# Two scanning layers on one core: the input on 128 partitions of 24 rows, kept in DRAM by position and quarter, the first eight rows placed by products, one group's input moved to a later place

## The chip, the core and the metric

The kernel runs on one core of a Trainium2 chip. The metric is the device time of one execution in microseconds (us), here the median of three runs. All data are 32-bit floats. Engines: PE multiplies matrices, DVE, ACT and POOL work element by element, SP only issues DMAs (ACT and POOL issue a few as well). Every engine takes its instructions in order, and an issuing engine stands still at a DMA whose data are not ready.

## What is computed

x has 32 images, 48 channels, 64 rows and 128 columns. There are two layers with weights of their own. Each normalizes x over 16 groups of three channels per image, runs four scans, and adds the result to x:

```
def layer(x, down, right, left):              # each a weight (48, 48, 5) and a bias
    v = (x - mean) / sqrt(var + 1e-5)         # per image and group of 3 channels, over all rows, columns
    for h in 1 .. 63:       D[h] = v[h] + conv5(D[h-1], down)          # along the columns
    U[63] = D[63]; then backwards with the same weights:
    for h in 62 .. 0:       U[h] = (D[h-1], or D[63] for h = 0) + conv5(U[h+1], down)
    for w in 1 .. 127:      R[w] = U[w] + conv5(R[w-1], right)         # along the rows
    for w in 126 .. 0:      L[w] = R[w] + conv5(L[w+1], left)
    return x + L
```

A row needs the row before it, so a scan is a chain of 63 or 127 steps. The statistics need all of an image's x before the first row can be scaled.

## The kernel before

**Groups and phases.** Eight images make a group; there are four. `PHASES` lists the order: row phases (down and up scan of one group, 126 steps) and column phases (right and left scan of two groups together, 254 steps). Twelve phases follow each other on PE without a break in the program: rows of group 0, rows of group 1, columns of both, and so on. The trace names a step by layer, group or pair, and way: `step_00d` is layer 0, group 0, down; `step_00r` layer 0, pair 0, right.

**A step** (`step`, L824) is nine matmuls (L837) over three partition groups o, and three additions on DVE (L846) that add the scan's input and the bias. In the trace a matmul is two records, so 63 steps are 1134 records. The 384 values of a row (eight positions of a column modulo 8, times 48 channels) are cut by `PIECES` into ten runs of 16 to 48 partitions. The arena holds three slots; rows 0 to 31 of a group lie in one, rows 32 to 63 in the next.

**From x to rows.** x arrives with channels and halves of the rows on 96 partitions (`PX`: channel c, half s), 32 rows on each. Bringing it into the layout of a step takes a round trip through DRAM for each row: `take_in` loads it, `permute` (L621, four copies of 96 x 256 on POOL or ACT) reorders it, `put_out` writes it to the DRAM tile `xin` in runs of 1 KB (`lines`), and `move_rows` reads it back in runs of 128 bytes, ten DMAs (one for each piece) for four or eight rows. `xin` has 96 lines, one for each partition, with 1024 elements of padding in every two of them (`PAD`), and inside a line the order is position (row modulo 8), quarter of the columns, block of eight rows. `scale_rows` (L667 on ACT, 24 instructions for four or eight rows) or `scale_at_once` (L678 on POOL) then normalize. The residual of layer 0 is read back from `xin` too (`load_residual`, runs of 4 KB).

**Statistics.** For group 0 DVE takes them (`InputStats.take`, L474, one for each 512 elements; `aggregate`, L477), for groups 1 to 3 ACT does (`take_others`, L487 and L495, sums and squares). `scaling` (L341) turns them into scale and offset with nine small matmuls on PE for x (L352, L363), a square root on ACT (L394) and a few DVE instructions.

**The start** (`first_group`, L1126) is written out by hand. It loads the first weights and builds the step's matrix from them with matmuls against shifted identities (`place_kernel`, L1180), loads group 0 in 16 pieces (two halves of the rows, eight images), takes statistics, and moves the rows. Rows 0 to 3 don't go through DRAM: `rows_by_product` (L1210) picks them from the loaded x by ten matmuls of 512 columns each with the shifted identities, and ACT copies the products from PSUM (L1217). After the scaling, `scale_first` normalizes rows 0 to 3 on DVE and ACT (L690, L692), then rows follow in the order in which `move_rows` and `scale_rows` stand. Puts and reads of `xin` alternate: rows 4 to 16 need the first half of the rows only.

**The order of everything else** is an agenda: `at(t, fn, ...)` sets work for step t, counted over all phases (`starts[k]` is a phase's first step), and `catch_up` writes it between the steps into each engine's instruction list. `in_order` keeps the instructions of an engine in the order in which they were written. `plan_input` sets the input of groups 1 to 3: for each piece of four rows a load, two permutes with their puts, and the statistics. Before, the third group's (index 2) eight pieces stand from step 16 of the first column phase on, 13.5 steps apart. The column phase holds four quarters of the columns in three slots: `plan_cols` writes quarter 0 away (`spill_unit`, steps 33 to 43 of the phase), loads quarter 3 in its place (`load_unit` with j = 3, steps 50 to 60), and reads quarter 0 back for the left scan. Nearly all these DMAs are on SP, so they stand in one line with the puts and loads of the input. Column 96 is the first of quarter 3.

Of the kernel before, what the change touches and what calls it, by code (L numbers as in the profile page):

```python
# [36 lines left out]
PX = 2 * C  # L37
# [83 lines left out]
def kernel(  # L121
# [22 lines left out]
    NBN = H * W // (2 * BN)  # L144
    CHANNEL = H * W * GB
    PAD = 1024
    WEIGHTS = NG * NG * FULL
    assert N == FULL and SLOT == NG * HALF * N and SLOT == 6 * UNIT

# [29 lines left out]
    mask_x = const([PX, PX], "mask_x")  # L179
    maskp = const([PX, NG, FULL], "maskp")  # L180
    mask_in = const([FULL, NG, C], "mask_in")
    mask_sb = mask_in[0:PX, 0]
    mask_r = const([FULL, NG, PX], "mask_r")
# [3 lines left out]
    def kept(name):  # L187
# [6 lines left out]
    MOIETY = (CHANNEL + PAD) // 2  # L194
    source = [
        [
            dram.tile([PX, MOIETY], F32, tag=f"xin{g}", name=f"xin{g}")[:, 0 : CHANNEL // 2]
# [29 lines left out]
    def x_by_row(t, e, h0, h1):  # L227

        s, h = divmod(h0, HALF)
        t = t.rearrange("(c s) (i q a e n) -> s e a c i q n", s=2, i=E8, q=NQ, a=NH // 2, e=E8)  # L230
        t = t[s, e, h // E8, :, h % E8 : h % E8 + h1 - h0]
        return t.rearrange("c i q n -> c (i q) n")

    def x_by_col(t, e, j):


        return t.rearrange("(c s) (i q n) -> i q c s n", s=2, i=E8, q=NQ)[e, j]

    def lines(t, h0, h1):

        t = t.rearrange("p (i q a n) -> a p i q n", i=E8, q=NQ, a=NH // 2)[h0 // E8]
        return t[:, h0 % E8 : h0 % E8 + h1 - h0].rearrange("p i q n -> p (i q) n")
# [70 lines left out]
    def load_masks(dma):  # L313
        for s in range(2):
            dma(sided(mask_sb)[s], mask[SIDES[s], SIDES[0]])
# [5 lines left out]
    def spread_masks():  # L321
        for s in range(2):
            nc.gpsimd.tensor_copy(mask_x.rearrange("p (c s) -> p s c", s=2)[:, s], mask_sb)
        for e, c0, c1, o, p0 in PIECES:
            nc.gpsimd.tensor_copy(maskp[:, o, p0 : p0 + c1 - c0], mask_sb[:, c0:c1])

    def spread_row_masks():
        for s in range(2):
            nc.gpsimd.tensor_scalar(
                mask_r.rearrange("p o (c s) -> p o s c", s=2)[:, :, s],  # L330
                mask_in,
                2.0 / E8,
                None,
                ALU.mult,
            )
# [5 lines left out]
    def scaling(key, layer, g, averages, masks, slack=0):  # L341
# [29 lines left out]
        average(ps[0:PX, 0], mean_p)  # L371
# [10 lines left out]
        dev = spare[0 : FULL if n > 1 else PX, 0:n]  # L382
        if not slack:
            far = ps[0:PX, 1 + NG : 2 + NG]
            nc.vector.tensor_tensor(far, mean_p, ps[0:PX, 0:1], ALU.subtract)
            nc.vector.tensor_tensor(dev, mean_p, ps[0:PX, 0:1], ALU.subtract)
# [20 lines left out]
        if n > 1:  # L407
            mean_c = stat_tile([PX, GB], "mean_c", key)
            nc.vector.tensor_copy(mean_c, ps[0:PX, 0])
            yield  # L410
            expand(mean, mean_c)
            yield
            nc.vector.tensor_tensor(dev, mean_p, mean, ALU.subtract)
            nc.vector.tensor_copy(mean_s, mean)
        else:
            nc.vector.tensor_tensor(dev, mean_p, ps[0:PX, 0:1], ALU.subtract)
# [8 lines left out]
        else:  # L425
            average(ps[0:PX, 1 + NG], dev, var_p)
            yield
            var_c = stat_tile([PX, GB], "var_c", key)
            nc.vector.tensor_copy(var_c, ps[0:PX, 1 + NG])
# [26 lines left out]
    class InputStats:  # L456
# [3 lines left out]
        def __init__(self, key, nv):  # L460
            self.nv = nv
            self.mv = stat_tile([PX, 1, GB, 2], "mv_x", key)
            if nv:
                self.st = stat_tile([PX, nv, NBN * 6], "bn", key)
            if nv < GB:
                self.sum, self.neg, self.dev2 = (
                    stat_tile([PX, GB, NBN], f"{n}_x", key)[:, nv:] for n in ("sum", "neg", "dev2")
# [11 lines left out]
        def take_others(self, i, nat):  # L479
            k = nat.shape[-1] // BN  # L480
            for square in (False, True):
                for b in range(self.nv, GB):
                    for n in range(k):
                        at = b - self.nv, slice(i + n, i + n + 1)
                        piece = nat[:, b, n * BN : (n + 1) * BN]
                        if square:
                            nc.scalar.activation(  # L487
                                junk[0:PX],
# [5 lines left out]
                        else:  # L494
                            nc.scalar.activation(  # L495
                                junk[0:PX],
# [8 lines left out]
        def __call__(self, key, slack):  # L505
# [3 lines left out]
            if self.nv < GB:  # L509
                n = GB - self.nv  # L510
                mean = stat_tile([PX, GB], "mean_x", key)[:, 0:n]
# [6 lines left out]
                    dev, dev, mean.unsqueeze(2).to_broadcast([PX, n, NBN]), ALU.add  # L518
# [7 lines left out]
                var = stat_tile([PX, GB], "var_x", key)[:, 0:n]  # L526
# [78 lines left out]
    def take_in(g, r0, nat, batches=slice(0, GB)):  # L605


        n = nat.shape[-1] // W
        src = x[g * GB : (g + 1) * GB].rearrange("b c (s h) w -> (c s) b (h w)", s=2)
        dma(nat[:, batches], src[:, batches, r0 * W : (r0 + n) * W])  # L610
# [12 lines left out]
    def put_out(g, r, perm):  # L623
# [3 lines left out]
        dma(lines(source[0][g], r, r + n), perm.rearrange("p (m n) -> p m n", n=LINE))  # L627
# [127 lines left out]
    def load_residual(k, j, i, nat):  # L755
# [3 lines left out]
        for e, c0, c1, p0 in pieces(o):  # L759
            here = nat[p0 : p0 + c1 - c0]  # L760
            if layer:
                dma(here, by_col(t, e, j)[c0:c1], nc.scalar)
            else:
                dma(here.rearrange("p (s n) -> p s n", s=2), x_by_col(t, e, j)[c0:c1])
# [336 lines left out]
    def wide_nat(i0, n):  # L1101
        return arena[0:PX, i0 : i0 + GB * n * W].rearrange("p (b m) -> p b m", b=GB)

    tiles = [stage[0:PX, i] for i in range(4)]
    nats1 = [wide_nat(2 * SLOT + i * UNIT * 2, 4) for i in range(4)]
    plan_input(1, [starts[0] + 46 + 6 * j for j in range(8)], 5, 1, nats1, tiles[2:4])
    nats = [wide_nat(3 * SLOT, 4)]
    times = [starts[2] + 16 + 13.5 * j for j in range(8)]
    plan_input(2, times, 6, 6, nats, tiles[2:4])
    times = [t + 15 * j for t in (starts[3] + 42, starts[4] + 24) for j in range(4)]  # L1110
# [5 lines left out]
    at(starts[1] + 58, load_row_masks)  # L1116
    at(starts[1] + 90, spread_row_masks)
# [8 lines left out]
    def first_group():  # L1126
# [4 lines left out]
        spare = {k: wt[k].rearrange("p i n -> p (i n)") for k in ("down1", "right", "left")}  # L1131
        to_row = [spare["right"][0:PX, i * FULL : (i + 1) * FULL] for i in range(9)]
        to_row += [spare["left"][0:PX, 0:FULL]]

        rows = HALF // 2
        parts = [wide_nat(SLOT + i * 2 * HALF * N * 2, rows) for i in range(2)]
# [3 lines left out]
        kernel = slot[slots(0)[0]][0:PX, 0 : TAPS * C + 6]  # L1140
        zeros = slot[slots(0)[0]][0:PX, 512 : 512 + NG * FULL + 6]

        def load_kernel():
            nc.vector.memset(kernel, 0.0)
            for j in range(TAPS):
                d, si = divmod(TAPS - 1 - j, 2)
                to = sided(kernel)[0][:, j * C : (j + 1) * C]
                dma(to, w[SIDES[si], 0, DOWN, d, SIDES[0]], nc.scalar if j % 2 else nc.sync)
            aside(sided(kernel)[0][:, TAPS * C :], bias[0:C].rearrange("c l k -> c (l k)"))

        def make_ident():
            nc.vector.memset(spare["right"], 0.0)
            nc.vector.memset(spare["left"][:, 0:FULL], 0.0)
            nc.vector.memset(zeros, 0.0)
            for m, (e, c0, c1, o, p0) in zip(to_row, PIECES):
                m = m[:, p0 : p0 + c1 - c0]
                nc.gpsimd.affine_select(
                    m,
                    m,
                    pattern=[[2, c1 - c0]],  # L1160
                    compare_op=ALU.not_equal,
                    fill=1.0,
                    base=2 * c0,
                    channel_multiplier=-1,
                )

        def place_kernel():
            for i in range(NG):
                ps = ps_rows.tile([FULL, BN], F32, tag=f"rows{i}", name=f"rows{i}")
                todo = [(to_row[0], zeros, slice(0, NG * FULL + 6))]  # L1170
                for m, (e, c0, c1, o, p0) in zip(to_row, PIECES):
                    if o == i:
                        for run in WEIGHT_RUNS:
# [14 lines left out]
        free = [spare["down1"][0:PX, 0:n]]  # L1188
        free += [
            row_views(0)[0][0:PX, o, h : h + 8].rearrange("p h n -> p (h n)")  # L1190
# [146 lines left out]
```

## Time and profile before

| | |
|---|---|
| median of three runs | 4242.22 us (4239.01 to 4245.74) |
| the profiled execution: its own time, its span | 4246.85 us, 4245.1 us |
| PE busy | 4072.4 us (96%), 36704 records |
| DVE, ACT, POOL busy | 2142.6, 1346.5, 870.8 us |
| first step of the first scan | 70.83 us |
| first up scan begins | 221.67 us |
| first column scan begins; its left scan | 605.71 us; 872.06 us |
| last matmul ends | 4165.86 us |
| PE's waits for the last statistics of group 0, and then for `scale_first` | 9.87 us, 6.53 us |
| DMA packets; under 512 B | 2129378; 2012497 |

A row of a timeline gives the start in the span, the time from there to the end of the last instruction of the row, engine, line, operation, what it writes and reads, the shape, how many instructions follow each other like this, and in brackets how long the engine had been idle and what ended the wait. A q behind the engine marks the sequencer that issues DMAs; its times are those of issuing, not of landing. A row of windows gives for each engine the busy time in the stretch, then the granted clock of PE, the share of the DMA engines that was busy, and GB/s. Before 75.9 us the trace has no record of the clock.

### The profile page before, as it was taken

How to read it: one execution, taken by the hardware profiler on the slowest of the kernel's cores; microseconds unless marked ns; L12 is line 12 of the kernel's file. 1: busy time of each engine (PE TensorE's matmuls, PEld its weight loads, DVE VectorE, ACT ScalarE, POOL GpSimd, SP SyncE). 2: the span in 40 equal slices, each digit the busy share in tenths (PEclk: the TensorE clock that was granted, in tenths of full speed). 3: DMA queues.
4: the chain of work that ended last, by engine and by line, in shares of the span. 5: the costliest groups of instructions: out<-in, count | busy, mean ns of one | idle time of the engine just before them, and what ended most of it. 6: DMA issues, size and time to landing. Idle time of an engine off the chain costs nothing. (4 is left out here: it accounts for less than half of the span.)

```text
span 4245.1 us, 90421 instructions
## 1 busy us (share of the span) xinstructions
PE 4072.4 (96%) x36704; PEld 4050.5 (95%) x36704; DVE 2142.6 (50%) x6517; ACT 1346.5 (32%) x2680; POOL 870.8 (21%) x879
## 2 busy tenths in 40 slices
PE   6999999899999999999999999999999999999992
PEld 5899999899999999999999999999999999999992
DVE  6454444457654454444447654444444444444443
ACT  4675001436885446000007863603000012110122
POOL 5460011334423020010014410000000024510352
PEclk9999999999999999999999999999999999999996
DMA  9999668868979999358409979839288049999999
GB/s 229 187 212 155 109 121 178 228 151 261 199 166 181 165 166 152 64 100 182 120 12 274 207 147 155 131 63 162 41 146 188 1 84 251 244 251 159 173 209 182
DMA packets 2129378, 679.80 MB, mean 160 GB/s; under 512 B 2012497, under 2 KB 2062913, under 8 KB 2095169
## 3 DMA queue, kind: packets, MB, share of 16 engines
q1 hardware_dynamic: 2026720, 582.07, 70.7%
q10 hardware_dynamic: 99680, 86.43, 9.5%
q8 instruction: 289, 4.73, 0.5%
q0 software_dynamic: 2560, 5.51, 0.5%
q14 instruction: 129, 1.05, 0.1%
HBM read 397.00 MB, written 295.14 MB: 163 GB/s over the span
## 5 line engine op out<-in xcount | busy, mean ns | idle before, releaser
L667 ACT ACTIVATE arena<-arena,offset,scale 128x256 f32<-128x256 f32 (+2 forms) x816 | 576.6, 800 | 355.0 <-DVE arena L846 122.1
L769 POOL TENSOR_TENSOR arena<-arena 128x2048 f32<-128x2048 f32 x80 | 363.0, 4553 | 1400.7 <-PE step_10l L837 437.5
L621 POOL COPY arena<-arena 96x256 f32<-96x256 f32 x452 | 267.5, 646 | 519.8 <-DMA arena<-in_x 481.0
L564 ACT ACTIVATE early<-arena 128x256 f32<-128x256 f32 x192 | 129.5, 675 | 450.6 <-POOL arena L769 444.5
L837 PE MATMUL step_00r<-arena,early 128*128 128x128 f32 x2286 | 253.6, 275 | 18.9 <-DVE arena L846 11.2
L837 PEld LDWEIGHTS step_00r<-arena,early 128*128 128x128 f32 x2286 | 252.9, 186 | 19.6 <-DVE arena L846 13.3
L837 PE MATMUL step_01r<-arena,early 128*128 128x128 f32 x2286 | 253.2, 274 | 9.6 <-DMA arena<-arena 5.8
L837 PEld LDWEIGHTS step_01r<-arena,early 128*128 128x128 f32 x2286 | 252.4, 186 | 10.3 <-issue 5.3
L837 PE MATMUL step_11r<-arena,early 128*128 128x128 f32 x2286 | 251.1, 273 | 5.2 <-DVE arena L846 5.2
L837 PEld LDWEIGHTS step_11r<-arena,early 128*128 128x128 f32 x2286 | 250.6, 185 | 5.6 <-DVE arena L846 5.6
L837 PE MATMUL step_00l<-arena,wleft 128*128 128x128 f32 x2286 | 249.1, 272 | 0.0
L837 PEld LDWEIGHTS step_00l<-arena,wleft 128*128 128x128 f32 x2286 | 248.6, 184 | 0.0
L837 PE MATMUL step_10l<-arena,wleft 128*128 128x128 f32 x2286 | 248.5, 272 | 0.0
L837 PE MATMUL step_10r<-arena,early 128*128 128x128 f32 x2286 | 248.5, 272 | 0.0
L837 PE MATMUL step_11l<-arena,wleft 128*128 128x128 f32 x2286 | 248.5, 272 | 0.0
L837 PE MATMUL step_01l<-arena,wleft 128*128 128x128 f32 x2286 | 248.4, 272 | 0.0
L837 PEld LDWEIGHTS step_10l<-arena,wleft 128*128 128x128 f32 x2286 | 248.4, 184 | 0.0
L837 PEld LDWEIGHTS step_10r<-arena,early 128*128 128x128 f32 x2286 | 248.4, 184 | 0.0
L837 PEld LDWEIGHTS step_11l<-arena,wleft 128*128 128x128 f32 x2286 | 248.4, 184 | 0.0
L837 PEld LDWEIGHTS step_01l<-arena,wleft 128*128 128x128 f32 x2286 | 248.4, 184 | 0.0
L794 ACT COPY arena<-arena 128x256 f32<-128x256 f32 x172 | 99.4, 655 | 400.9 <-POOL arena L769 136.9
L261 ACT COPY early<-arena 128x1 f32<-128x1 f32 x2 | 0.4, 192 | 657.3 <-DVE arena L846 657.3
(203 smaller groups left out, 7163.7 us busy)
## 6 DMA issues: line engine op xcount, KB each, us to landing
arena<-in_x SPq DMA_DIRECT2D x24, 1536.0 KB, 11.6
xin<-arena SPq DMA_DIRECT2D x48, 768.0 KB, 5.4
arena<-xin SPq DMA_DIRECT2D x96, 384.0 KB, 8.2
mid<-arena SPq DMA_DIRECT2D x96, 384.0 KB, 7.7
arena<-mid SPq DMA_DIRECT2D x192, 192.0 KB, 4.3
upb<-arena SPq DMA_DIRECT2D x192, 192.0 KB, 3.9
arena<-upb SPq DMA_DIRECT2D x96, 384.0 KB, 12.1
arena<-xin SPq DMA_DIRECT2D x186, 192.0 KB, 4.3
```

Source lines behind the costliest of these rows:

```text
L261: fn(*args)
L564: nc.scalar.activation(junk[:, 0:n], view[:, b], AF.Identity, accum_out=self.sum[:, i, j : j + 1])
L621: copy(dst[:, r, q], src[:, r0 + r, q])
L667: nc.scalar.activation(args[0], args[0], AF.Identity, bias=args[2], scale=args[1])
L769: eng.tensor_tensor(unit, unit, nat, ALU.add)
L794: copy(by_w(perm)[:, a], src[:, a])
L837: nc.tensor.matmul(part(whole(ps[o])[0:m], -s), weights[:, i, at : at + m], part(src(i), s), start=seen[o] == 1, stop=seen[o] == left[o],)
```

## The change

x is cut into 128 partitions of 24 rows: an image's 48 x 64 rows in order, 24 for each partition, so that eight partitions hold one group of three channels. The masks for the statistics become blocks of eight partitions and are made on POOL (`blocks`, `make_masks`) instead of loaded. Loads of group 0 stay 16, of 12 rows and one image each, with as many bytes as before; statistics are 48 instead of 64 instructions. Groups 1 to 3 come in six pieces of four rows instead of eight.

`xin` is laid out as position and quarter first (32 of them), then channels, then 2048 elements: no padding, and the residual of one position and quarter is one run per channel of 8 KB. A put (`x_put`) writes one row of every partition, in runs of 1 KB; there are 24 for a group instead of 32 rows. A put's row belongs to one position for all channels, and to a block of rows that changes with the partition.

The first eight rows, instead of four, come by products: they are loaded a second time, in channel order (`top`, rows 0 to 3 on partitions 0 to 47 by SP, rows 4 to 7 on partitions 64 to 111 by ACT), ahead of the 16 loads. The products are 20 of 512 columns instead of ten, from 48 partitions instead of 96. Seven of them stand after the scaling on PE, ahead of the first step. The identities become two shifted ones in the memory of the left weights.

The third group's pieces move from step 16 to step 60 of the first column phase; those of the second group to step 44 of the first phase, 7.5 apart; row masks are loaded at step 20 instead of 58 of the second phase.

```diff
-    MOIETY = (CHANNEL + PAD) // 2
-            dram.tile([PX, MOIETY], F32, tag=f"xin{g}", name=f"xin{g}")[:, 0 : CHANNEL // 2]
+            dram.tile([E8 * NQ, C, UNIT], F32, tag=f"xin{g}", name=f"xin{g}")
...
+    def x_put(t, r):
+        t = t.rearrange("(i q) c (a n) -> i (c a) q n", i=E8, a=NH)[r % E8]
+        return t.rearrange("(p r) q n -> r p q n", r=PR // E8)[r // E8]
...
+    def blocks(t, n):
+        nc.vector.memset(t, 1.0 / E8)
+        for base, step in ((0, 1), (E8 - 1, -1)):
+            nc.gpsimd.affine_select(
...
-        src = x[g * GB : (g + 1) * GB].rearrange("b c (s h) w -> (c s) b (h w)", s=2)
-        dma(nat[:, batches], src[:, batches, r0 * W : (r0 + n) * W])
+        src = x[g * GB : (g + 1) * GB].rearrange("b c h w -> b (c h w)")
+        src = src.rearrange("b (p m) -> p b m", p=FULL)
+        dma(nat, src[:, :, r0 * W : (r0 + n) * W])
...
-    plan_input(1, [starts[0] + 46 + 6 * j for j in range(8)], 5, 1, nats1, tiles[2:4])
+    plan_input(1, [starts[0] + 44 + 7.5 * j for j in range(6)], 5, 1, nats1, tiles[2:4])
-    times = [starts[2] + 16 + 13.5 * j for j in range(8)]
+    times = [starts[2] + 60 + 13.5 * j for j in range(6)]
-    times = [t + 15 * j for t in (starts[3] + 42, starts[4] + 24) for j in range(4)]
+    times = [t + 15 * j for t in (starts[3] + 42, starts[4] + 24) for j in range(3)]
-    at(starts[1] + 58, load_row_masks)
-    at(starts[1] + 90, spread_row_masks)
+    at(starts[1] + 20, load_row_masks)
+    at(starts[1] + 40, spread_row_masks)
...
+        order = [*range(0, 4), *range(8, 12), *range(4, 8), *range(16, 20)]
+        order += [*range(12, 16), *range(20, 24)]
...
+        def rows_by_product(s, o):
+            src = top[SETS[s][0] : SETS[s][1]]
...
         load_kernel()
+        for s, (p0, p1) in enumerate(SETS):
+            src = x[0:GB].rearrange("b c h w -> c b (h w)")
+            dma(
+                top[p0:p1],
+                src[:, :, s * four * W : (s + 1) * four * W],
+                nc.scalar if s else nc.sync,
+            )
...
         for b in range(GB):
             stats.take(0, parts[0], b)
-        put_rows(0, 4, 8, free, pool, act)
-        rows_by_product(0, 4)
-        put_rows(0, 8, 14, free, pool, act)
-        put_rows(0, 14, 16, free, pool)
-        move_rows(0, 4, 8, False)
-        move_rows(0, 8, 16, False)
+        put_rows(pool, act, pool, act)
+        rows_by_product(0, 0)
+        put_rows(pool, act, pool, act)
+        rows_by_product(0, 1)
+        put_rows(pool, act, pool)
+        rows_by_product(0, 2)
+        put_rows(pool)
+        rows_by_product(1, 0)
         for b in range(GB):
             stats.take(NBN // 2, parts[1], b)
             stats.aggregate(b)
+        put_rows(act, pool)
         for _ in scaling("x0", 0, 0, stats, x_masks):
             pass
         scale_first(0, 4, 5)
+        put_rows(pool, act, pool, act)
+        rows_by_product(1, 1)
+        rows_by_product(1, 2)
+        move_rows(0, 8, 12, False)
+        put_rows(pool, act, pool, pool, pool, pool)
+        move_rows(0, 12, 16, False)
         scale_rows(0, 4, 8)
-        scale_rows(0, 8, 16)
-        put_rows(1, 0, 8, free, pool)
-        move_rows(0, 16, 24, False)
-        scale_rows(0, 16, 24)
-        put_rows(1, 8, 16, late, pool)
-        move_rows(0, 24, 32, False)
-        scale_rows(0, 24, 32)
-        put_rows(0, 0, 4, later, pool)
-        move_rows(0, 32, 40, False)
-        scale_rows(0, 32, 40)
-        move_rows(0, 40, 64, False)
+        scale_rows(0, 8, 12)
+        scale_rows(0, 12, 16)
+        for h in range(16, 64, 8):
+            move_rows(0, h, h + 8, False)
+            if h < 40:
+                scale_rows(0, h, h + 8)
```

## The prediction

> **What bounds the kernel now.** I read the page first. PE is busy 96% of the span, evenly, and the steps are serial (step h needs row h-1), so a wait of PE is worth its own length wherever it stands, and work on another engine is worth nothing unless PE waits for it. Then the order of PE's records, which shows where it stands still: before the first step (70.83 us), in the first down scan, in the first column scan, and after the last step (79 us, not touched). A scan without a wait shows the pace: the 63 steps from 350.54 take 124.5 us, 1.975 us each; a column scan of 127 steps takes 248.4 us.
>
> PE's timeline (start, length, engine, line, operation, tiles, shape, count, idle before and what ended it):
> ```profile
> 31.12 16.71 PE L1210 MATMUL rows<-arena,early 96*128 96x512 f32 x18 [7.57 <-DMA arena<-in_x]
> 47.65 2.00 PE L1210 MATMUL rows<-arena,wleft 96*128 96x512 f32 x2
> 59.52 0.46 PE L352 MATMUL ps_x<-mv_x_x,mask_x 96*96 96x8 f32 x2 [9.87 <-DVE mv_x_x L477]
> 60.93 1.42 PE L363 MATMUL ps_x<-dev_x,maskp 96*128 96x8 f32 x6 [0.94 <-DVE dev_x L388]
> 62.86 1.45 PE L363 MATMUL ps_x<-mv_x_x,maskp 96*128 96x8 f32 x6 [0.51 <-ACT std_x L394]
> 70.83 0.77 PE L837 MATMUL step_00d<-arena,early 128*128 128x128 f32 x2 [6.53 <-DVE arena L690]
> 71.98 9.81 PE L837 MATMUL step_00d<-arena,early 128*128 128x128 f32 x70 [0.39 <-DVE arena L690]
> 84.75 0.49 PE L837 MATMUL step_00d<-arena,early 128*128 128x128 f32 x2 [2.96 <-DVE arena L846]
> ...
> 221.67 71.26 PE L837 MATMUL step_00u<-arena,early 128*128 128x128 f32 x648
> ...
> 605.71 16.98 PE L837 MATMUL step_00r<-arena,early 128*128 128x128 f32 x126 [6.05 <-DMA arena<-arena]
> 624.34 174.52 PE L837 MATMUL step_00r<-arena,early 128*128 128x128 f32 x1604 [1.65 <-DMA upa<-arena]
> 810.09 62.14 PE L837 MATMUL step_00r<-arena,early 128*128 128x128 f32 x556 [11.23 <-DVE arena L846]
> ```
> PE waits for the last statistics (9.87 us), then for scaling; in the down scan it waits for adds (L846). What those wait for stands on ACT's timeline (scalings without a gap), and what paces the statistics on DVE's (one load of 786,432 bytes per 3.15 us):
> ```profile
> 76.34 21.00 ACT L667 ACTIVATE arena<-arena,offset,scale 128x64 f32<-128x64 f32 x46 [2.82 <-DMA arena<-xin]
> ...
> 109.42 11.32 ACT L667 ACTIVATE arena<-arena,offset,scale 128x128 f32<-128x128 f32 x22 [3.04 <-DMA arena<-xin]
> ```
> ```profile
> 21.55 2.47 DVE L474 BATCH_NORM_STATS2 bn_x<-arena 96x6 f32<-96x512 f32 x4 [0.68 <-DMA arena<-in_x]
> 24.71 2.47 DVE L474 BATCH_NORM_STATS2 bn_x<-arena 96x6 f32<-96x512 f32 x4 [0.69 <-DMA arena<-in_x]
> ```
> The down scan ends where the up scan starts: it took 150.8 us where 124.4 are needed, and the right scan 266.4 where 248.4 are. The wait of 11.23 us is at column 96, where the last quarter (load_unit, j = 3) begins. SP's own order says why it was late:
> ```profile
> 714.33 1.11 SPq L250 DMA_DIRECT2D xin<-arena  x2
> 717.12 4.30 SPq L250 DMA_DIRECT2D arena<-in_x  x1
> 721.51 4.59 SPq L250 DMA_DIRECT2D spill<-arena  x1
> 740.25 0.30 SPq L250 DMA_DIRECT2D xin<-arena  x1
> ```
> From 726 to 740 SP stands at a put of the third group's input, whose permute waits for its own load; spills and the quarter's loads are queued behind it. Last, how fast loads can be: the window row of the input load (its last two numbers are DMA share and GB/s), and the GB/s of 985 to 999 us in 40 slices, where three spills come back on 128 partitions:
> ```profile
> 10.00:31.00 21.00, 13.55 (x57) 12.69 (x55) 16.08 (x27) 1.09 (x4) 1.94 (x12) 1.00 1.02 250
> ```
> ```profile
> GB/s 234 222 246 246 281 304 304 316 363 386 410 398 468 398 445 468 398 421 398 468 398 445 468 398 421 375 445 421 445 398 398 375 304 257 234 140 70 47 0 0
> ```
>
> **The change part by part: load and statistics.** The 16 loads stay at 786,432 bytes but lie on 128 partitions; two loads of the same size (top, eight rows in channel order) are added ahead. Rate of a 128-partition load: at best the spills' 425 GB/s, 1.85 us each; at worst unchanged, 3.15. I take 2.1, near the spills because the shape is theirs except for 6 KB runs. The first statistics started at 8.80, so loading began to count at 8.8 - 3.15 = 5.6 us, so the first half has landed at 5.6 + 10 x 2.1 = 26.6 and the second at 43.4 us (57 before). Statistics: 48 instead of 64 at 0.617 (2.47 / 4); the second half is eight times 3 x 0.617 + 0.37 + gaps, 18.3 us from 28.7, so they end at 47.0 (59.4 before).
>
> **TensorE before the first step.** Placing the kernel is the same 39 matmuls, to 23.5 us. The products double, 10 to 20. Ten took 18.7 us, so 1.85 each: 13 of them stand ahead of the scaling, 23.6 + 24.1 = 47.7. TensorE and statistics meet there. The scaling's last matmul came 4.9 us after the statistics (59.4 to 64.3); add 0.2 because one ACT permute (2.3 us, from 48.7 to 51.0) stands ahead of its square root: 52.8. Seven products follow, on the path: 13.0, so 65.8. The scaling of rows 0 to 3 (L690, 6.17 us) would be done at 60.3 and hides behind them. First step at 65.8 instead of 70.83: 5.0 us won of 12.4.
> Here a rule bears on the sum. The Trainium skill ("TensorE: Matmul & The Clock Gate", Part 1: The HAM clock gate) says that about 3.4 us of sustained matmuls bring the full clock. By it the 20 products would cost 18 us less. But the row shows 0.91 us per record of 512 columns from first to last of 18 us, 1.8 ns a column, against 174.52 / 1604 = 0.109 us for 128 in the scan, 0.85 ns: half speed throughout, with 96 rows in use; the new ones use 48. The row decides; the rule's case is a rival below.
>
> **ACT in the scan.** Its prices: 22 scalings of 128x128 took 11.32, 0.515 each; the 46 hold 24 of those, leaving 8.6 for 22 of 128x64, 0.39 each. ACT after the last product: copy to 66.7, a permute to 69.0, then 24 for rows 4 to 7: 78.4; rows 8 to 11: 87.8; 12 to 15: 97.2; 16 to 23: 109.6; 24 to 31: 122.0. PE needs 11.0 us for its first four steps (70.83 to 81.79, half clock at first): 76.8; row 4 is there at 78.4, row 8 at 87.8 (PE asks at 86.6), row 12 at 97.2 (96.0), row 16 at 109.6 (105.4). From there 48 steps: 94.8. With 3 us for half-clock stretches after these waits the scan ends near 208 instead of 221.7: 13.7 won. The new waits are small, and ACT is what is late next.
>
> **The round trip.** Every partition now holds three rows of each position (h modulo 8), so reading rows 8 to 11 back needs puts among the first sixteen, and rows 12 on need all 24, which before came piece by piece. SP stands at the puts of ACT's permutes with these reads queued behind it. The last permute on ACT ends at 69.0, its puts (1.35 us each: 0.52 MB at the 375-390 GB/s of the puts before) land near 78; rows 8 to 11 have landed near 71, 12 to 15 at 84, 16 to 23 at 95, against ACT's 78, 88 and 97. Hidden by 2 to 7 us. This needs the old reading rate: 32 rows were issued in 40.33 us from 136.68, so 10 to 11 us per eight rows, 12 where mixed. The new position-first layout has no pad, and its pitches (8 KB between channels, 384 KB between quarters, 1.5 MB between positions, for 128-byte runs) appear in no row. Below: a gain isn't excluded, the residual now reads whole 8 KB runs. Above: the Trainium skill ("DMA: Bandwidth & Descriptors", Latency and other measured facts) reports copies at half rate when partitions lie megabytes, a large power of two, apart, cured by a few KB of pad. By it eight rows cost 22 us, by the row 11. I take the row, since partitions are 8 KB apart here and no pitch but that is a power of two, and keep 22 as the other end.
>
> **Third group's input, later.** Its pieces move from step 16 to step 60 of the right scan, six instead of eight. Ahead of column 96 only one load (2.1 MB, about 7 us of DMA) is left of four, and no put: 3 x 1.57 MB and eight puts of 0.79 MB leave, and SP's stop of 14 us with them. The quarter is needed at 793 us (605.7 + 1.65 + 95 x 1.955). Its spills can start when the quarter before has landed, near 712; six take 18 us, 20 loads 30 and the one input load 7: near 767. The 11.23 us go, with about 1.3 of the half-clock stretch behind them: 12.5. What is late next: puts end at step 137, the residual loads want the tiles at 143, and their first use is at 161. If that cover failed it would cost POOL, not PE, up to 35 us.
>
> **At nothing:** 32 puts become 24 per group (permutes a quarter fewer, 0.65 us each) and ACT's 128 statistics per later group become 96, all beside PE's scans; masks made on POOL (a dozen operations of 0.2) instead of loaded lie under the input load; row masks moved to step 20 of the second scan lie on an SP with slack. If hidden no longer, the masks cost 2 to 3 us.
>
> **Sum.** 13.7 + 12.5 = 26.2. The profiled execution took 4246.85 (span 4245.1): 4220.6. The median of the runs is 4.6 lower, so 4216.
>
> **The rivals.**
> - *Half speed isn't kept, or seams gain too* (0.17): with products at 0.92 the step starts at 58.4, ACT is only 4 us earlier, scan end 204; some of the 10 us that each scan of the third group loses (134 instead of 124.4) goes with fewer DMAs. 4208.
> - *The load doesn't speed up* (0.14): 18 x 3.15 + 5.6 = 62.3, statistics 64.5, everything 17 us later, scan end 225; only the columns gain. 4233. For it: shorter runs; against: the spills' GB/s.
> - *Slower: reading back at the new pitch* (0.06). Reads start at 65; seven chunks of x us and 5 us of puts, then the two POOL scalings (6.7 each) and eight steps: end at 99 + 7x. It takes over from x = 15.6 and eats the whole gain at x = 19.3, 75% above today. At 23: end 260, 4268.
> - The likeliest has 0.56; the rest are mixtures within the range.
>
> **Numbers.** A run can tell about 0.2%, 8.5 us. Faster 0.91, same 0.05 (load rival and part of the reading), slower 0.04. Range 4203 to 4233.
>
> **What would show it.** Statistics ending at 47 rather than 59; first step near 66 with products right ahead of it; small waits at rows 4 and 16; up scan starting near 208; no wait at column 96; reads of xin still near 11 us per eight rows. Wrong if input loads stay at 250 GB/s, or if PE waits on DMA from xin in the down scan.

## The result and the profile after

The changed kernel took 4222.03 us (median of nine runs, 4211.96 to 4228.38) against 4239.01 us before (nine runs on the same chip, 4233.29 to 4246.21): ratio 0.9956, 95% interval 0.9942 to 0.9969, 17 us less. A second measurement of the same kernel (`after_again`, below) gave 0.9944 (0.9931 to 0.9956), 24 us less. Forecast were 4216 us, within 4203 to 4233, and a gain of 26 us. The mechanisms named came about, some with other sizes, and some microseconds were lost in places that the sum did not have.

PE's timeline of the profiled execution (4228.38 us; span 4226.6), the rows that answer to those shown of before:
```profile
22.88 20.54 PE L1243 MATMUL rows<-arena,wleft 48*128 48x512 f32 x26
44.40 0.57 PE L363 MATMUL ps_x<-mv_x_x,mask_x 128*128 128x8 f32 x2 [0.99 <-POOL arena L637]
...
49.23 13.10 PE L1243 MATMUL rows<-arena,wleft 48*128 48x512 f32 x14
62.27 10.94 PE L856 MATMUL step_00d<-arena,early 128*128 128x128 f32 x72
74.23 0.49 PE L856 MATMUL step_00d<-arena,early 128*128 128x128 f32 x2 [1.02 <-DVE arena L865]
...
98.07 10.35 PE L856 MATMUL step_00d<-arena,early 128*128 128x128 f32 x72 [5.65 <-DVE arena L865]
111.46 0.49 PE L856 MATMUL step_00d<-arena,early 128*128 128x128 f32 x2 [3.04 <-DVE arena L865]
...
207.05 53.16 PE L856 MATMUL step_00u<-arena,early 128*128 128x128 f32 x483
...
609.42 236.54 PE L856 MATMUL step_00r<-arena,early 128*128 128x128 f32 x2160 [3.74 <-DVE arena L865]
```
The wait of 9.87 us for the statistics is 0.99, the first step comes at 62.27 instead of 70.83 with the products right ahead of it, and the up scan starts at 207.05 instead of 221.67. So 8.6 us are won before the first step and 6.0 in the down scan. Before, the scan had waits at row 4 (2.96 us, shown with the prediction) and at rows 8, 16 and 24:
```profile
96.76 0.49 PE L837 MATMUL step_00d<-arena,early 128*128 128x128 f32 x2 [1.65 <-DVE arena L846]
120.22 0.80 PE L837 MATMUL step_00d<-arena,early 128*128 128x128 f32 x2 [6.60 <-DVE arena L846]
141.19 0.80 PE L837 MATMUL step_00d<-arena,early 128*128 128x128 f32 x2 [2.94 <-DMA arena<-xin]
```
Now it has 1.02, 5.65 and 3.04 us at rows 4, 12 and 16. In the right scan nothing stands between 609.42 and the left scan at 845.80: the wait at column 96 is gone. The largest wait that is left, before row 12, is new in this place. ACT's timeline says why:
```profile
65.06 18.93 ACT L688 ACTIVATE arena<-arena,offset,scale 128x64 f32<-128x64 f32 x48
85.79 0.51 ACT L688 ACTIVATE arena<-arena,offset,scale 128x64 f32<-128x64 f32 x1 [1.80 <-DMA arena<-xin]
```
From 84.0 us on ACT waits for the loads of rows 12 to 15 (twice more, until 89.7), and its scalings of them end at 99.4. SP's order in that stretch:
```profile
63.63 6.18 SPq L249 DMA_DIRECT2D arena<-xin  x10
69.91 3.46 SPq L249 DMA_DIRECT2D xin<-arena  x4
...
82.21 69.96 SPq L249 DMA_DIRECT2D arena<-xin  x70
```
The last six puts are issued behind the loads of rows 8 to 11; the 24th lands at 82.16, and only then do the other 70 loads start. They go on at 1.0 us each, ten for four or eight rows, as fast as before: reading position first costs nothing here. DVE's last statistics, and the window row of the input load:
```profile
43.94 0.32 DVE L488 BATCH_NORM_AGGREGATE mv_x_x<-bn_x 128x2 f32<-128x36 f32 x1
```
```profile
10.00:41.00 31.00, 31.00 (x80) 19.00 (x79) 28.38 (x50) 13.36 (x26) 15.31 (x27) 1.00 1.01 410
```
410 GB/s against 250: a load of 786,432 bytes lands every 1.88 us, and the statistics end at 44.3 instead of 59.4. (The 1.00 in the row's clock column is no measurement: the first clock record of this profile stands at 68.07 us.) SP's rows around the last quarter hold no put any more, only six spills, 6 and 14 loads, and one input load; the last of them:
```profile
717.99 23.83 SPq L249 DMA_DIRECT2D arena<-upa  x14
```
The last load lands at 753 us, 31 us before PE comes to column 96 (609.42 us and the 174.52 that the profile before shows from there).

Where the time went, from the starts of the scans in two profiles of each kernel (the second ones are the experiments `before_again` and `after_again`):

| stretch | before, again | after, again | predicted | mean difference |
|---|---|---|---|---|
| to the first up scan | 221.67, 222.10 | 207.05, 206.60 | -13.7 | -15.1 |
| to the first column scan | 384.04, 383.26 | 381.16, 381.79 | 0 | -2.2 |
| first column scans | 516.97, 516.63 | 508.33, 503.55 | -12.5 | -10.9 |
| third group's scans (02d, 02u) | 268.54, 262.68 | 270.41, 268.12 | 0 | +3.7 |
| to the last right scan | 2270.02, 2270.09 | 2271.53, 2267.02 | 0 | -0.8 |
| from there to the end | 583.9, 587.9 | 588.1, 589.8 | 0 | +3.1 |
| span | 4245.1, 4242.7 | 4226.6, 4216.9 | -26.2 | -22.2 |

### The profile page after: what moved, and what is told of

It reads as the page before. It is cut to its first block, busy times and chain, and to the rows that moved or that the text cites. A ratio compares the mean times of both kernels' runs of the same rounds, so it can differ in the third digit from the quotient of the medians.

```text
span 4226.6 us, 90155 instructions
## 1 busy us (share of the span) xinstructions
PE 4086.4 (97%) x36724; PEld 4055.0 (96%) x36724; DVE 2135.8 (51%) x6501; ACT 1287.5 (30%) x2525; POOL 791.2 (19%) x737
## 5 line engine op out<-in xcount | busy, mean ns | idle before, releaser
L637 POOL COPY arena<-arena 128x256 f32<-128x256 f32 x332 | 196.7, 660 | 443.1 <-DMA arena<-in_x 394.2
L856 PEld LDWEIGHTS step_01r<-arena,early 128*128 128x128 f32 x2286 | 253.3, 187 | 10.9 <-DVE arena L865 6.0
```

Source lines behind the costliest of these rows:

```text
L637: copy(dst[:, r, q], src[:, r0 + r, q])
L856: nc.tensor.matmul(part(whole(ps[o])[0:m], -s), weights[:, i, at : at + m], part(src(i), s), start=seen[o] == 1, stop=seen[o] == left[o],)
```

## The experiments

My theory after the result: in the first stage the faster loads and the scalings' earlier start win the 15 us, and would win more if the puts did not land late; in the columns SP's stop is gone; the rest varies from execution to execution. The rival: the change itself causes the losses behind column 127, by its new layout of `xin` or by the later input.

**The same kernels again.** `after_again` is the changed kernel unedited.

> The kernel after, unchanged, to see what of its losses behind column 127 belongs to the change and what to the execution. If they belong to the change: again 3.7 us of waiting near column 8 of the first right scan, 6.5 us of issue wait in the third group's down scan and a tail of 82.8 us, each within 0.5. If they vary from execution to execution: the first scan repeats to 0.5 us (up scan at 207), but these three move by 2 us or more, with the total at 4212 to 4229.

Measured: 4218.64 us, ratio 0.9944 (0.9931 to 0.9956), up scan at 206.60. The wait near column 8 is 0.89 us instead of 3.74: it varies. The wait in 02d, near row 33, is 5.96 (6.46), and the tail from the last matmul to the end of the span 83.1 us (82.8): these two repeat. `before_again` is the kernel before.

> The kernel before, unchanged, for a second profile of it. What varies from one execution to the next, if the view is right that column 8, the seams and the tail vary and the waits of the first scan and of column 96 don't: up scan at 219 to 223, a wait of 9 to 12 us at column 96; the down scan of the third group, 134.1 us in the first profile, and its up scan, 134.4, may move by 2 us or more.

Measured: 4244.45 us (one run); up scan at 222.10, 11.50 us of waiting at column 96, 02d 131.6 us and 02u 131.1. Its tail is 81.1 us, 79.2 in the first profile; over all twelve profiles of experiments it lies between 78 and 88 us, in kernels that share everything there, so I count it as variation. The wait near row 33 of 02d is 0.85 in this profile and 2.91 in the first one of before.

**The columns.** `late_only` makes one edit in the kernel before:
```diff
-    times = [starts[2] + 16 + 13.5 * j for j in range(8)]
+    times = [starts[2] + 60 + 9.5 * j for j in range(8)]
```


> The kernel before with one thing of the change: the third group's input starts at step 60 of the right scan instead of 16 (eight pieces, 9.5 steps apart, so that the last one stands at step 126.5; 110.5 before). Own theory: SP no longer stands at puts while the last quarter's loads are queued, so the wait of 11.23 us at column 96 goes; the first stage is untouched (up scan still starts near 221.7). About 9 to 11 us less than before, 4229. Rival (a later third group costs the scans that read it): the columns gain the same, but the third group's down scan waits for its scaling 6 us longer, so 3 to 5 us less in all, 4235. Second rival (the wait is the loads' own rate): no change, the wait stays at 8 to 11 us.

Measured: 4236.45 us, 0.9987 (0.9975 to 1.0000). The wait at column 96 is gone; PE's timeline from 780 to 870 us, in which that column falls, is one row without idle time:
```profile
779.81 90.45 PE L837 MATMUL step_00r<-arena,early 128*128 128x128 f32 x831
```
The two column scans take 509.6 us instead of 517.0 and 516.6; near column 8 PE waits 4.5 us in this profile, against 1.65 and 1.17. In the profiled execution 00u took 134.1 us (128.9, 128.2), with a wait of 3.79 us at 299 us, where this edit has done nothing yet. So the mechanism holds, with 7 us in the two column scans. The whole shows about 6, with an interval from nothing to 11, which by itself decides little. The first rival's total fits, its place doesn't: 02d took 135.5 us (134.1, 131.6). From there the reverse in the changed kernel, `early_again`:
```diff
-    times = [starts[2] + 60 + 13.5 * j for j in range(6)]
+    times = [starts[2] + 16 + 18.9 * j for j in range(6)]
```


> The kernel after with the third group's input back at step 16 of the right scan (six pieces, 18.9 steps apart, so that the last one stands at 110.5 as in the kernel before). Own theory: the first stage stays as in the kernel after (up scan starts near 207), and a wait of 8 to 11 us comes back at column 96: 4222 + 9 = 4231. Rival 1 (the late start gives its gain back in the third group's scans): the wait comes back, but the third group's down scan is 6 us shorter: 4225. Rival 2 (a quarter fewer puts is what cured column 96, not the start): no wait, 4222.

Measured: 4220.13 us, 0.9947 (0.9935 to 0.9960), and no wait at column 96. My theory expected it back; the second rival seemed right. But I had also spread the pieces. `early_dense` keeps them 13.5 apart:
```diff
-    times = [starts[2] + 60 + 13.5 * j for j in range(6)]
+    times = [starts[2] + 16 + 13.5 * j for j in range(6)]
```


> The kernel after with the third group's input at step 16 of the right scan and its pieces 13.5 steps apart, so that only its start differs from the kernel after. If fewer and shorter puts alone cure column 96 (as with 18.9 steps apart, where the last load of the quarter landed 5 us before it was asked for): no wait there, the last of the 20 loads lands 3 us or more before column 96, at 180 to 189 us from the scan's start. If the start does it: a wait of 3 to 11 us at column 96, the last load at 194 or later.

Measured: 4221.88 us (one run). The wait is back, in PE's timeline:
```profile
790.32 59.88 PE L856 MATMUL step_00r<-arena,early 128*128 128x128 f32 x534 [9.85 <-DVE arena L865]
```
and in SP's the puts stand in front of the quarter's loads again:
```profile
747.39 1.08 SPq L249 DMA_DIRECT2D xin<-arena  x2
750.54 0.37 SPq L249 DMA_DIRECT2D arena<-in_x  x1
750.97 28.18 SPq L249 DMA_DIRECT2D arena<-upa  x17
```
17 of 20 loads wait until 751 us, and the last lands at 790. So fewer puts alone cure nothing; what counts is how much input stands in SP's order ahead of the quarter, and both a later start and wider steps take it away. And yet the whole is no slower than the kernel after: from the left scan to the end of 02u it took 515.7 us, against 521.2 and 518.9. Taken together, from the first column scan to the end of 02u, it took 780.5 us, against 778.7 and 771.7 in the kernel after and 785.5 and 779.3 before. So what the later input wins at column 96 is partly given back in 02d, and what is left of it is no larger than what two profiles of one kernel differ by.

**The layout of xin.** In all ten profiles with the layout of the change and the later or spread input, PE waits 2.4 to 9.4 us near row 33 of 02d; in the three with the old layout 0.3 to 2.9. In the kernel after:
```profile
1166.42 0.77 PE L856 MATMUL step_02d<-arena,early 128*128 128x128 f32 x2 [6.46 <-issue]
```
The profile names no releaser here, so the data have to be followed back. The step needs row 32. ACT's scalings of rows 32 to 47 wait for the loads of these rows from `xin`:
```profile
1142.98 0.86 ACT L688 ACTIVATE arena<-arena,offset,scale 128x256 f32<-128x256 f32 x1 [7.39 <-DMA arena<-xin]
```
They are 20 loads, the first of a block of 23 in SP's order (the other three are of the residual), before:
```profile
1146.89 26.25 SPq L250 DMA_DIRECT2D arena<-xin  x23
```
and after:
```profile
1119.23 31.20 SPq L249 DMA_DIRECT2D arena<-xin  x23
```
Counted from the scan's first step, the last of these 20 loads lands at 50.7, 48.6 and 48.0 us in the three profiles of the old layout and at 50.3 to 57.4 us in the ten. `early_dense`, which has the new layout too, has 48.3 us and waits only 0.54. In all fourteen profiles the wait is the landing time less 47.9 us, to within 0.2 us, and ACT's 24 scalings of these rows end 16.5 to 16.7 us after the landing. So the late landing of these rows makes the wait. What makes them land late?

In part the loads are slower. The 20 that follow (rows 48 to 63) took 24.7, 22.2 and 23.3 us in the three profiles of the old layout, and 25.3 to 26.5 in the eleven of the new one. Is it the pitch, as the rule in the prediction would have it in a small way? `padded` puts 4 KB behind each quarter, `channel_pad` 128 bytes behind each 1 KB, so that channels are 9 KB apart:
```diff
-            dram.tile([E8 * NQ, C, UNIT], F32, tag=f"xin{g}", name=f"xin{g}")
+            dram.tile([E8 * NQ, C * UNIT + PAD], F32, tag=f"xin{g}", name=f"xin{g}")[
+                :, 0 : C * UNIT
+            ].rearrange("p (c n) -> p c n", c=C)
```
```diff
-            dram.tile([E8 * NQ, C, UNIT], F32, tag=f"xin{g}", name=f"xin{g}")
+            dram.tile([E8 * NQ, C, NH, UNIT // NH + 32], F32, tag=f"xin{g}", name=f"xin{g}")[
+                :, :, :, 0 : UNIT // NH
+            ]
```


> The kernel after with 4 KB of pad behind each quarter of x in DRAM, so that quarters lie 388 KB and positions 1.52 MB apart instead of 384 KB and 1.5 MB. Own theory (channels 8 KB apart set the rate, or nothing does): no change, 20 loads back of the second and third groups stay at 21 to 22 us each and 25 to 26 in the third group's scan, PE's wait in that scan at 4.5 to 6.5 us. Rival (the pitch of quarters and positions makes the reading slower): the 20 loads of the third group fall to 23 to 24 us and the wait to 1 to 3 us as in the kernel before.

> The kernel after with 128 bytes of pad behind every 1 KB of x in DRAM, so that channels lie 9 KB apart instead of 8 KB (the residual is then read in runs of 1 KB). In the eight profiles so far that read x by position and quarter, PE waits 4.5 to 8.9 us near row 33 of the third group's down scan, in the two of the old layout 1.0 and 2.9; the last 20 loads of that group were issued in 25 to 26.5 us against 22 and 25. If the pitch of 8 KB makes the reading slower: 22 to 24 us for those 20, the 40 loads of the second group in 40 to 41 us instead of 42.5 to 44, the wait at 1 to 3 us. If it doesn't (the wait comes from when these loads stand in SP's order): 25 us or more, 42.5 to 44, the wait at 4.5 us or more.

Measured (one run each): 4236.76 and 4238.77 us; the 20 loads took 26.1 and 26.3 us, the 40 of the second group 42.5 and 42.3, the wait was 5.84 and 9.44 us. Neither pad changes the rate, so neither pitch by itself is the cause. Nor is the block's own time enough to tell the wait: it took 27.4 us in `early_dense` and 27.7 in `channel_pad`, but the one began 20.0 us after the scan's first step and the other 29.4, and the waits are 0.54 and 9.44 us. So it is when the block starts, together with how long it takes. What shifts its start in SP's order, and what makes the loads slower, the runs left open.

**The input load.** What made it faster, 128 partitions instead of 96, or the distance in DRAM, 12 KB from partition to partition instead of 16? (The expectation says 32; with 32 rows of 512 bytes on a partition it was 16.)
```diff
-                dma(parts[i][:, b], flat(b)[:, i * rows * W : (i + 1) * rows * W])
+            for p0, p1 in ((0, 96), (96, FULL)):
+                for b in range(GB):
+                    src = flat(b)[p0:p1, i * rows * W : (i + 1) * rows * W]
+                    dma(parts[i][p0:p1, b], src)
```


> The kernel after with each half of the input loaded as eight loads of partitions 0 to 95 (589,824 bytes each) and then eight of partitions 96 to 127 (196,608 bytes each), the addresses in DRAM as they were (12 KB from partition to partition, 6 KB runs; the kernel before had 32 KB and 8 KB). What made a load 1.88 us instead of 3.15? If the number of partitions: 250 GB/s as before, so a load of 96 partitions lands every 2.36 us, and the first stage becomes some 16 us longer or more. If the distance in DRAM (32 KB then, 12 KB now): 418 GB/s stays, every 1.41 us, and the first step comes at most 8 us later, since the statistics of the first half start later.

Measured: the windows of this kernel while loads of 96 partitions ran, and then of 32 (last number GB/s):
```profile
13.08:28.56 15.48, 15.48 (x50) 11.25 (x51) 0.00 (x0) 1.09 (x4) 0.00 (x0) 1.00 1.02 263
28.56:36.10 7.54, 7.54 (x10) 2.69 (x9) 6.64 (x12) 0.00 (x0) 0.00 (x0) 1.00 1.01 210
```
It is the partitions. Seven loads of 589,824 bytes took 15.48 us, 2.21 each, so three quarters of the bytes take longer than all of them on 128 partitions (1.88). That these loads are smaller does not explain it: the kernel before moved the full 786,432 bytes on 96 partitions at 250 GB/s. The DMA share reads 1.0 in both windows: it tells that engines are busy, not that they move much. The Trainium skill ("SBUF — State Buffer", Door 1: The DMA port swizzle) counts ports reached: 32 partitions reach 8 of 16, about 218 GB/s, and the row's 210 agrees. 96 partitions reach all 16, 64 of them over 8 ports; if those set the time, 96/128 of the full rate would be left, an estimate of 308 from the 410 measured. The rows show 263, so ports alone do not give it. The first step came at 89.62 us, the up scan at 230.47, 8.8 us later than in the kernel before, and the whole took 4240.71 (one run). The two column scans keep their gain here (503.9 us), but without the loads' shape the first stage is slower than before, and nothing of the whole is left.

**The middle of the first scan.** `few_products` cuts the seven products on the path to two:
```diff
+            if s == 1 and o > 0:
+                mine = mine[:1]
```


> The kernel after with the last seven products cut to two: rows 4 to 7 lack the channels of the other five, so that part of the computation is left out. Own theory (after the change the loads of rows 12 to 15 behind the 24th put set the middle of the first scan, the products only its start): the first step comes at 59.7, where rows 0 to 3 are scaled, 2.6 us earlier, but the wait at row 12 grows by nearly the same, and the up scan starts at 205 to 207. Rival (ACT's chain, which starts after the products, sets it, as the prediction had it): ACT starts its scalings at 56 to 58, 8 us earlier, and the up scan starts 5 us or more earlier, below 202.

Measured: 4225.04 us (one run), up scan at 204.85. PE's timeline:
```profile
98.24 11.02 PE L856 MATMUL step_00d<-arena,early 128*128 128x128 f32 x72 [8.44 <-DVE arena L865]
```
The first step came at 57.87, after a wait for the scaling of rows 0 to 3. Of the 4.4 us won there, 2.2 are left at the end of the scan: row 12 starts at 98.24 instead of 98.07, whatever comes before it. So behind row 8 it is not the products' end that counts. Then ACT or the loads? `pool_rows8` takes rows 8 to 11 from ACT:
```diff
-        scale_rows(0, 8, 12)
+        scale_at_once(0, 8, 12, nc.gpsimd)
```


> The kernel after with rows 8 to 11 of the first group scaled by POOL instead of ACT, in the old order of puts and loads. Own theory (ACT's chain and the late loads of rows 12 to 15 together make the waits at rows 12 and 16): rows 8 to 11 landed at 72, POOL needs 2 x 3.43 us, so it has them at 79, before TensorE asks (83); ACT is free at 74.5 and takes rows 12 to 15 as they land, to 91, rows 16 to 23 to 103; of 5.65 and 3.04 us at most 2 are left, and the up scan starts near 199 instead of 207. 4211 to 4214 in all. Rival (the loads of rows 12 to 15 alone decide, ACT doesn't): row 12 still waits 4 us or more, up scan at 204 to 207.

Measured: 4222.52 us, 0.9956 (0.9941 to 0.9971), up scan at 207.33, 5.75 us at row 12. The rival is right:
```profile
86.96 0.51 ACT L688 ACTIVATE arena<-arena,offset,scale 128x64 f32<-128x64 f32 x1 [11.64 <-DMA arena<-xin]
```
ACT idles 11.64 us, then starts on rows 12 to 15 when their loads land (90 us) and needs its 9.7 us behind that; I had counted these as overlapping. `puts_first` sets the six puts ahead of the loads of rows 8 to 11 and gives these rows to POOL:
```diff
-        move_rows(0, 8, 12, False)
         put_rows(pool, act, pool, pool, pool, pool)
+        move_rows(0, 8, 12, False)
         move_rows(0, 12, 16, False)
         scale_rows(0, 4, 8)
-        scale_rows(0, 8, 12)
+        scale_at_once(0, 8, 12, nc.gpsimd)
```


> The kernel after with two moves in the first stage: the six last puts stand on SP ahead of the loads of rows 8 to 11, and rows 8 to 11 are scaled by POOL, which is idle then, instead of ACT. Own theory (after ACT's chain, what is late is the 24th put, landed at 82.2, and the loads of rows 12 to 15 behind it, for which PE waits 5.65 us at 98.1 and 3.04 at 111.5): the 24th put lands near 75, rows 8 to 11 land near 80 and POOL has them at 84, rows 12 to 15 land near 86 and ACT has them by 92; at most 2 us of the two waits are left, the up scan starts at 200 instead of 207, 4216 in all. Rival (the loads' own rate or POOL is the bound): row 8 waits 5 us or more for POOL, the up scan starts at 205 to 209, no change.

Measured: 4220.20 us, 0.9941 (0.9928 to 0.9955), up scan at 203.54, between the two forecasts. The 24th put lands at 77.1 instead of 82.2 and the waits at rows 12 and 16 are gone, but row 8 now waits 5.71 us for POOL, whose first of two operations starts at 83.9, when the loads of rows 8 to 11 have landed:
```profile
83.93 3.43 POOL L699 TENSOR_TENSOR arena<-arena,scale 128x1536 f32<-128x1536 f32 x1 [20.63 <-DMA arena<-xin]
```
`puts_split` shares the scalings:
```diff
+        put_rows(pool, pool, pool, pool, pool, pool)
         move_rows(0, 8, 12, False)
-        put_rows(pool, act, pool, pool, pool, pool)
...
-        scale_rows(0, 8, 12)
-        scale_rows(0, 12, 16)
+        scale_rows(0, 8, 12, 1)
+        scale_at_once(0, 8, 12, nc.gpsimd, 1)
+        scale_rows(0, 12, 16, 2)
+        scale_at_once(0, 12, 16, nc.gpsimd, 2)
```
(the last argument splits the three partition groups o between ACT and POOL.)

> The kernel after with the first stage's middle changed by what the runs before showed: all six last permutes on POOL, their puts ahead of the loads of rows 8 to 11 on SP, rows 8 to 11 scaled by ACT (one third) and POOL (two thirds), rows 12 to 15 by ACT (two thirds) and POOL (one third). Own theory (the 24th put and the scalings behind the loads of rows 8 to 15 make the waits): no wait at row 4, 2 to 4 us at row 8, at most 2 us later; the up scan starts at 197 to 200 instead of 207, and the whole is 4211 to 4214. Rival (one of the loads is late whatever the order): up scan at 203 or later, and no difference to the kernel after.

Measured: 4225.15 us, 0.9959 (0.9946 to 0.9972), up scan at 203.75, not 197 to 200:
```profile
87.74 17.90 PE L856 MATMUL step_00d<-arena,early 128*128 128x128 f32 x142 [5.77 <-DVE arena L865]
```
No wait at row 4, but the 24th put still lands at 76.4, rows 8 to 11 land by 82.3, and row 8 waits. (Row 16 waits 3.04 us more.) The puts' landing and the loads behind them are the bound of the middle; the order only chooses which row pays. Both versions start the up scan at 203.5 to 203.8, against 205.6 to 207.1 in the four profiles whose first stage is that of the kernel after unedited, and neither can be told from the kernel after in the whole.

## Why the prediction held, step by step

- **Loads and statistics:** right in kind, 1.88 us instead of 2.1, so the end is 44.3 instead of 47.0. `loads_96` shows that the reason given (the spills' shape, 128 partitions) was the right one.
- **Products:** seven on the path, 13.0 predicted, 13.10 measured. Of the 13 ahead of the scaling the records are 0.91 us apart as said, up to 37.6 us; then, for 3.8 us, two lie beside each other in each 0.91. That ended the 13 at 43.4 rather than 47.7, and PE waits for the statistics. With both, the first step came 3.5 us earlier than said (62.3, not 65.8). By the rule of the clock gate that the prediction cites, all of them would have gone at the fast pace, and the seven would have taken half of 13.1. The row was the better guide: 14.7 us of products without a pause, from 22.9 to 37.6 us, kept 0.91. The scan's own matmuls did change pace: their records go from 0.21 us apart to 0.11 at 68.1 us (75.9 before), 5.8 us after the first step (5.1 before), and the first clock record of each trace, full clock, stands at that moment. Whether the few rows, the 512 columns or something else kept the products slow, no run tells.
- **ACT's chain and the round trip:** here the step failed, and another error hid it. The sum had puts landed near 78 and rows 12 to 15 at 84, "hidden by 2 to 7 us"; they landed at 82.2 and 89.6, and ACT waits. The end of ACT's rows 12 to 15, said to be 97.2 by ACT's own chain, is 99.4 by the loads' (`few_products`, `pool_rows8`). What would show the prediction wrong, a wait for `xin` in the down scan, happened. The up scan still came at 207.05, 208 being forecast, because two errors met: ACT's chain began at 65.1 instead of 69.0, and would have had rows 12 to 15 some 6 us before 99.4 by its own pace, had the loads not held it up. That the number fits is luck here.
- **Reading back at the new pitch:** the rival that the kernel gets slower is refuted by 70 loads in 69.96 us. In 02d the last loads do take 11% longer; two pads did not move that, so its cause is open.
- **Columns:** 12.5 predicted, 10.9 measured in the column scans. That puts ahead of the quarter in SP's order make the wait was right as the mechanism (`late_only`, `early_dense`); the wait near column 8 (3.74 and 0.89 us in the kernel after, 1.65 and 1.17 before) adds its variation. That the whole gets shorter by this part is not shown clear of noise.
- **The sum:** 26.2 against 22.2 in the profiles, and 17 and 24 between the medians of the two measurements. The term that was not in it is the third group's scans, +3.7 in the mean, though the two profiles of before differ by 5.9 there. Its down scan alone is clear: 131.6 to 135.5 us in the three profiles of the old layout, 137.7 to 146.0 in the nine with the new layout and the input at step 60, 135.2 and 135.9 in the two with the new layout and the input at step 16. This is a cover that I had priced at nothing: that `xin`'s loads for rows 32 to 47 land before ACT needs them. They stand in SP's order behind the residual's loads and the results' puts (from 1008 to 1202 us the profile after shows no pause over 1.1 us in that order). What comes of the layout and what of the later input stays open: `late_only` has the later input and no loss, `early_dense` the new layout and no loss, and of each there is one profile. The 2.2 us won ahead of the first column scan and the 3.1 lost at the end were not in the sum either; the second I count as variation.

## What to carry to other kernels

Look at how many partitions a load reaches before anything else: here 128 instead of 96 took a load of equal size from 3.15 to 1.88 us, while the DMA engines read as fully busy in both. When a layout makes a read depend on all puts instead of some, put the landing of the last put into the sum, and what stands ahead of it in the queue: here the 24th put landed at 82.2 us, 17 us after the last permute ended. And where a wait is won in one stage, look at the next stage of the same queue: here 10.9 us were won in the columns and 3.7 lost in the scans behind them. Where two profiles of one kernel differ by as much, judge from more than one.

## What was not expected of the hardware

Loads on 96 partitions (2.21 us for 589,824 bytes, 263 GB/s) take longer than a whole load of 786,432 bytes on 128 (1.88 us), and this is not explained by the ports alone. And products from 48 partitions can overlap: where the first ones from partitions 64 to 111 meet the last from 0 to 47, two records of 1.09 us each lie beside each other, ten in 5.8 us instead of 9.1, at the same time in ten of the eleven profiles of the new layout; in the other, `loads_96`, the second set started later, at 41.3 us, and all 26 kept 0.91. That they share the array in this way is what the records suggest; it was not tried by itself.
